# V and K of twelve sequences per class-split layer, moved into the wait for the split; transfers issued later

## The chip, the core and the metric

The kernel runs on one core of a Trainium2 chip. The metric is the device time of one execution in microseconds; a result is the median of several executions. Every trace is of one execution, taken by the hardware profiler.

## What is computed

Sixteen sequences (B) of 512 tokens (S) with 256 channels (C) go through four attention layers, each of the form x = x + attention(layernorm(x)), with 16 heads of 16 dimensions. The order is `PLAN = ("a", "f", "b", "f")`:

```python
x = x + attn_a(layernorm(x))   # causal mask, biases on q, k, v
x = x + ffn(layernorm(x))      # "f": attention within two classes of tokens
x = x + attn_b(layernorm(x))   # rotary positions, no mask
x = x + ffn(layernorm(x))      # "f" again, same weights

# in an "f" layer:
sim = (qg_n * q_n).sum(-1).mean(-1)              # cosine of each token's q with a fixed direction
sim = (sim - sim.min()) / (sim.max() - sim.min())  # over ALL tokens of ALL sequences
pos = sim > 0.9                                  # two classes; the first 5 tokens belong to both
# each token attends to the tokens of its own class and the first 5
```

The 16 sequences of an "f" layer are one batch row set of the same call, so the minimum and the maximum couple them: no product of an "f" layer can start before `sim` of all sixteen sequences is known. This is the class split.

## The kernel before

**Work units.** A quad is one layer, one sequence b and four heads (g = 0 to 3): 256 quads, 64 to a layer. For a quad TensorE (PE) makes the score product twice. First `maxima.score` (tile `s`, L610) gives scores with queries on the partitions, from which VectorE (DVE) takes a row maximum (L619, or the masked L626 in layer 0); the maxima are turned, split in two and written through DRAM (`md`, L654) into extra rows of the quad's Q operand (L657, GpSimd queue). Then `products.score` (tile `t`, L687) gives the shifted scores with keys on the partitions, ScalarE (ACT) takes the exponential (L702) and `weigh` (tile `po`, L713) multiplies with V; `o` (L729) evicts the quad's result. The maxima run 20 score steps (`AHEAD`), that is two and a half quads, ahead of the products.

**Operands through DRAM.** Q and K of a sequence are kept in DRAM (`qd`, `kd`) as high and low parts, V in `vd`. `prep(layer, b, x)` makes them: layernorm (`stats`, `begin`), transposition (`normed`, tile `xp`) into x^T with a high and a low part (`xh`, `xl`), then six-matmul projections for V (`values`, L467, two halves), Q and K (`parts`, L360, two halves each). Each half of Q or K is split into two parts in a tile of a pool of two buffers (`t`, tag "parts": `tq`, `tk`) and sent by four transfers from the SP queue (`send`, L370 and L374). In an "f" layer `prep` also makes `sim` (`similar`, `similarity`): on GpSimd by a power (L432), on ScalarE and VectorE for the last sequence. `constant_rows(b)` (L245) writes 16 constant rows of `qd` and `kd` per head from DRAM, once for each sequence. `load_quad` (L577, GpSimd queue) brings one quad's Q and K into one of five buffers.

**Order.** PE's order is written out by the program: a main loop over the quads calls `advance` (maxima), `score` and `weigh`, and between them `fill_in` runs steps of background generators (`prep`, `tail`, `masked`, `registers`) by a planner with made-up costs and due times (`yield wait, cost`). `tail(layer, b)` divides, projects and adds to x, then pushes `prep(layer + 1, b)`. So while layer n runs its products, layer n + 1 is prepared. The other engines' and queues' orders are set by a scheduler that plays the program through; SP and GpSimd issue their transfers strictly in that order.

**The transition to an "f" layer.** After the last quad of layers 0 and 2 the loop drains all background work (tail of sequence 15, prep of 14 and 15) and calls `split(layer + 1)`: global extremes, classes, four flag rows per sequence to DRAM (`fd`), and from there 64 transfers (L568) into rows of `qd` and `kd` of all sixteen sequences. Then the quads of the "f" layer are loaded, 20 score steps of maxima run, and the first product `t` follows.

Of the kernel before, what the change touches and what calls it, by code (L numbers as in the profile page):

```python
# [63 lines left out]


TURN, ONE, TWO, POOL = 107, 2400, 4000, 6000
ROWS = 48
# [52 lines left out]
def hybrid_kernel(ctx: ExitStack, tc: tile.TileContext, a: dict, out: bass.AP):  # L120
# [4 lines left out]
    def pool(name, bufs, **kw):  # L125
# [5 lines left out]
        pool("w", 2),  # L131
# [15 lines left out]

    def load_const(name, shape, pool_=None):
        t = (pool_ or const).tile(shape, F32, tag=name, name=name)
        nc.sync.dma_start(t, a[name])  # L150
        return t
# [12 lines left out]
    xd = [dram.tile([P, NT, C], F32, tag=f"xd{b}", name=f"xd{b}") for b in range(B)]  # L164
    fd = dram.tile([4, B, S], F32, tag="fd", name="fd")
# [3 lines left out]
    def load_x(layer, b):  # L169
        t = p3.tile([P, NT, C], F32, tag="x", name=f"x{layer}_{b}")  # L170
        src = a["x"][b].rearrange("(t p) c -> p t c", p=P) if layer == 0 else xd[b]
        nc.sync.dma_start(t, src)
        return t
# [7 lines left out]

    def load_weights(layer, project):

        kind = PLAN[layer]
        ws = (WO,) if project else (WQ, WK, WV)
        tag = "o" if project else "q"
        wp = pwo if project else wpool
        wh = wp.tile([P, 2, len(ws), C], FR, tag="wh" + tag, name=f"wh{tag}{layer}")
        wl = wp.tile([P, 2, len(ws), C], FR, tag="wl" + tag, name=f"wl{tag}{layer}")
        for i in ws:  # L190
            raw = ptmp.tile([P, 2, C], F32, tag="tmp", name=f"wraw{layer}_{i}")
            nc.sync.dma_start(raw, a[f"{kind}_w"][:, :, i, :])
            if i in (WQ, WK):
                by_parity = ptmp.tile([P, 2, C], F32, tag="tmp", name=f"wpar{layer}_{i}")
                nc.vector.tensor_scalar(
                    by_parity.rearrange("p c (i e m) -> p (c i) e m", i=2, e=2),
                    raw.rearrange("p c (i m e) -> p (c i) e m", i=2, e=2),
                    SCALE if i == WQ else 1.0,
                    None,
                    ALU.mult,  # L200
                )
                raw = by_parity
            k = 0 if project else i
            nc.scalar.copy(wh[:, :, k, :], raw)
            nc.vector.tensor_tensor(wl[:, :, k, :], raw, wh[:, :, k, :], ALU.subtract)
        return wh, wl

    def broadcast_row(name):
        t = const.tile([P, C], F32, tag=name, name=name)
        nc.sync.dma_start(t, a[name].partition_broadcast(P))  # L210
        return t
# [30 lines left out]
    def constant_rows(b):  # L242
        for w, d in ((0, qd[b]), (1, kd[b])):
            for e in range(2):
                nc.sync.dma_start(d[e, ROWS:], a["zo"][w].unsqueeze(1).to_broadcast([HALF - ROWS, H // 2, S]))  # L245
# [36 lines left out]
    def late_constants():  # L282
        late["later"] = load_const("later", [P, P])
        for kind in ("a", "f"):
            bo[kind] = broadcast_row(f"{kind}_bo")
        late["regs"] = load_const("regs", [P, 3, B * NT])
        late["hm"] = load_const("hm", [P, 2 * H])
        late["blk"] = load_const("blk", [P, H, HV])
        late["half"] = load_const("half", [P, REG])
        for t in rst:  # L290
            nc.gpsimd.memset(t.bitcast(F32), 0.0)
            for e in range(2):
                r = HALF * e + ROWS + 2
                nc.gpsimd.dma_start(t[r : r + 2], a["rows"][e])
        late["cos"] = load_const("cos", [P, S])
        late["sin"] = load_const("sin", [P, S])
        direction()


    def prep(layer, b, x):  # L300
# [35 lines left out]
        def normed(u):  # L336
# [12 lines left out]
            if u == 0:  # L349
                xn(2)  # L350
                xn(3)

# [65 lines left out]
        def similarity():  # L418
# [7 lines left out]
            if b == B - 1:  # L426
# [29 lines left out]
        def values(u):  # L456

            v = vst[b % 2]
# [24 lines left out]

        yield 0, 0
# [16 lines left out]
        for u in range(2):  # L501
            yield lag, 1380
            values(u)
            lag = 0
        if kind == "b":
            for w in "qk":
                for i in range(2):
                    yield (8000 if w == "k" and i == 0 else 0), 1362
                    half_turned(w, i)
                turned(w)  # L510
        elif kind == "a":
            for w in "qk":
                for i in range(2):
                    yield 0, 1362
                    parts(w, i)
        else:
            for w, i in ("q0", "q1", "k0"):
                yield 0, 1362
                parts(w, int(i))
            yield 0, 1750  # L520
            similar()
            yield 0, 1362
            parts("k", 1)
            yield 0, 260
            similarity()
        busy["prep"] -= 1
# [4 lines left out]
    def split(layer):  # L531

        n = B * NT
# [11 lines left out]
        nc.vector.tensor_scalar(dg, ident[:2, :2], mm, None, ALU.mult)  # L545
        pb = small(f"mb{layer}")
# [11 lines left out]
        nc.vector.tensor_tensor(fl[:, 3, :], pos, regs[:, 1, :], ALU.mult)  # L558
        pf = small(f"pf{layer}")
# [5 lines left out]
        for b in range(B):  # L565
            for k, d in ((0, qd[b]), (2, kd[b])):
                for e in range(2):
# [3 lines left out]
                    )  # L571


    def load_quad(i):
        layer, b, g = quads[i]
        for t, d in ((Qs[i % NB], qd[b]), (Ks[i % NB], kd[b])):
            nc.gpsimd.dma_start(t, d[:, :, 2 * g : 2 * g + 2, :].rearrange("e r h s -> (e r) h s"))  # L577
# [12 lines left out]
    def maxima(quad):  # L590
# [10 lines left out]
        def score(t, p):  # L601
# [6 lines left out]
            for e in range(2):  # L608
                r = slice(HALF * e, HALF * e + n_rows)
                nc.tensor.matmul(  # L610
# [123 lines left out]
    def registers(layer, b):  # L734
# [80 lines left out]
        def first():  # L815
            yield (lambda: b == 0 or (layer, b - 1) in NEG), 0
# [3 lines left out]
        def rest():  # L820
            yield (lambda: (layer, b, 0) in registered), 0
# [10 lines left out]
    busy = {"norm": False, "prep": 0, "layers": set(), "first": 0}  # L832
    prepared, registered, summed, tailed, put = set(), set(), set(), set(), set()
    divided = set()
# [36 lines left out]
    def tail(layer, b):  # L871
# [59 lines left out]
        def can():  # L931
# [5 lines left out]
                and (b < 2 or layer + 1 == len(PLAN) or (layer + 1, b - 2) in prepared)  # L937
# [61 lines left out]
    def push_call(f, after=None):  # L999
        def gen():  # L1000
            yield (lambda: busy["prep"] == 0 and (not after or after in tailed)), 0
# [4 lines left out]
    def drain(credit=None, until=None):  # L1006

        while fill and not (until and until()):
            now = clock["now"]
            able = [s for s in fill if s.ready <= now and (s.next == 0 or banks[0] <= now) and s.open()]  # L1010
            if not able:
                if credit is not None:
                    return
# [30 lines left out]
    def prep0(b, x=None):  # L1044
        push(prep(0, b, load_x(0, b) if x is None else x), 2)
        busy["first"] += 1
        constant_rows(b)

    prep0(0, first_x)
    early_constants()  # L1050
# [5 lines left out]
    def advance(to, budget=0):  # L1056

        while taken["n"] < to:
# [10 lines left out]
            if budget:  # L1069
                at = clock["now"]  # L1070
                drain({"ns": budget})
                clock["now"] = max(clock["now"], at + budget)

    waiting = None
    for i, (layer, b, g) in enumerate(quads):
# [4 lines left out]
        if b or g or layer:  # L1080
# [15 lines left out]
        if kind == "a" and g == 1:  # L1096
            push(masked(b), 2)
        if b == 0 and g == NG - 1 and layer + 1 < len(PLAN):
            push_call(lambda layer=layer: W.__setitem__(layer + 1, load_weights(layer + 1, False)))
        if b == 0 and g == NG - 2:  # L1100
            push_call(lambda layer=layer: WP.__setitem__(layer, load_weights(layer, True)), layer and (layer - 1, B - 1))
        if alone:
            advance((2 * NT) * i + AHEAD, 900)
        if i not in put:
            drain(until=lambda: i in put)
        score, weigh = products(i)
        for t in range(NT):
            for p in range(2):
# [3 lines left out]
                if p == 0:  # L1112
                    fill_in(layer)
                elif waiting:
# [5 lines left out]
            if i == 0:  # L1120
                load_through(i + 4) if t == NT - 1 else None
            waiting = lambda weigh=weigh, t=t: weigh(t)
        if kind != "f" and b == B - 1 and g == NG - 1 and layer + 1 < len(PLAN):
# [3 lines left out]
            drain()  # L1127
            split(layer + 1)
# [46 lines left out]
```

## Time and profile before

| | |
|---|---|
| three timed executions | 4234.24, 4244.86, 4248.88 us; median 4244.86 |
| the profiled execution | 4242.52 us, span 4240.7 us |
| busy in the span | PE 3937.4 (93%), DVE 3207.0 (76%), ACT 2631.8 (62%), POOL 1820.8 (43%) |
| mean granted TensorE clock | 0.946 of full speed |
| DMA | 661.84 MB, mean 156 GB/s; mean busy shares of the 16 engines between 0.2 and 1.0 by stage |
| last eviction `o` of layer 0, first product `t` of layer 1 | 1272.5 and 1381.65 us |
| last eviction `o` of layer 2, first product `t` of layer 3 | 3291.4 and 3408.7 us |
| first product `t` of layer 0 | 100.4 us |

Times are from the start of the span. PE is matrix multiplication, PEld its weight loads; POOL is GpSimd; SPq is the SP queue that issues transfers. In a view by windows each row holds the busy time of an engine and in brackets its instructions, then the granted TensorE clock, the mean busy share of the 16 DMA engines and what they moved. The chain of waits is the one path of work that ended last, each row a start, a length and a line.

### The profile page before, as it was taken

To read this page: it belongs to the slowest core of one execution; us is meant where nothing else is said; L and a number is where in the kernel's file an instruction comes from. 1 tells how busy PE (TensorE), PEld (TensorE's weight loads), DVE (VectorE), ACT (ScalarE), POOL (GpSimd) and SP (SyncE) were. 2 spreads that over 40 slices of the span, in tenths; PEclk is the share of its full clock that TensorE was granted. 3 is DMA by queue.
4 is the path that set the end of the run, shared out by engine and by line. 5 is a ranking of instruction groups with operands and counts; after the bars stand their busy time and mean duration, and the time that the engine had idled before them with its cause. 6 is when DMAs were issued, how large, how long until landed. Compare 5 with 4: busy or idle time off the path is not lost.

```text
span 4240.7 us, 79626 instructions
## 1 busy us (share of the span) xinstructions
PE 3937.4 (93%) x27440; PEld 2051.1 (48%) x27440; DVE 3207.0 (76%) x7488; ACT 2631.8 (62%) x5288; POOL 1820.8 (43%) x2421
## 2 busy tenths in 40 slices
PE   3899999999995999999999999999999599999999
PEld 2565656565553444444444444444444334444444
DVE  4676776667654888888888788888886389999996
ACT  1444454444452777777777667777777267777777
POOL 2124545354543256656665634444444412222221
PEclk6899999899996999999999999999999689999999
DMA  9556566666645345555554645455554623333331
GB/s 300 160 159 187 182 200 181 189 184 190 193 128 167 96 137 170 163 149 165 171 162 152 186 146 169 146 167 168 164 157 126 188 85 114 122 116 114 119 121 51
DMA packets 294722, 661.84 MB, mean 156 GB/s; under 512 B 51624, under 2 KB 90032, under 8 KB 294320
## 3 DMA queue, kind: packets, MB, share of 16 engines
q1 hardware_dynamic: 204080, 384.02, 28.9%
q0 software_dynamic: 90240, 272.73, 21.6%
q8 instruction: 219, 3.59, 0.3%
q14 instruction: 183, 1.50, 0.1%
HBM read 379.46 MB, written 298.06 MB: 160 GB/s over the span
## 4 chain that ended last, share of the span: by engine, by line
PE 72%; DVE 10%; DMA 7%; SPq 3%; ACT 3%; issue 3%; POOL 2%; ACTq 0%; DVEq 0%; POOLq 0%
PE po L713 19%; PE s L610 15%; PE t L687 11%; DVE mx L619 5%; PE pv L467 5%; PE pj L922 4%; PE pq L360 4%; DMA qd<-tq 3%; PE pk L360 3%; PE ot L884 2%; POOL nd L432 2%; DVE sc L626 1%; PE rs L759 1%; PE t L698 1%; SPq L568 1%
## 5 line engine op out<-in xcount | busy, mean ns | idle before, releaser
L702 ACT ACTIVATE e<-t 128x512 f32<-128x512 f32 (+2 forms) x3840 | 2017.6, 588 | 824.2 <-PE t L687 538.6
L619 DVE TENSOR_REDUCE mx<-s 128x1 f32<-128x512 f32 x3072 | 1944.4, 681 | 334.7 <-PE s L610 326.2
L610 PE MATMUL s<-ks,qs 52*128 52x512 f32 (+4 forms) x4096 | 1030.8, 481 | 92.3 <-DMA ks<-kd 78.1
L687 PE MATMUL t<-qs,ks 52*128 52x512 f32 (+4 forms) x4096 | 1000.2, 402 | 103.5 <-ACT e L702 35.5
L713 PE MATMUL po<-e,v 128*32 128x512 f32 (+1 forms) x8192 | 1031.1, 576 | 5.1 <-ACT o L729 3.9
L610 PEld LDWEIGHTS s<-ks,qs 48*128 48x128 f32 (+1 forms) x4096 | 429.9, 191 | 1085.7 <-ACT e L702 310.9
L687 PEld LDWEIGHTS t<-qs,ks 50*128 50x128 f32 (+1 forms) x4096 | 496.8, 191 | 302.3 <-DVE mx L619 102.6
L626 DVE CUSTOM_DVE_ANT_0 sc<-s,mask_s_bf 128x128 bf16<-128x128 f32 (+3 forms) x1024 | 497.7, 486 | 160.5 <-PE s L610 78.6
L577 POOL DMA_DIRECT2D qs<-qd x256 | 153.6, 601 | 811.5 <-PE t L687 530.7
L657 POOL DMA_DIRECT2D qs<-md x512 | 268.5, 529 | 543.7 <-DMA md<-ms 516.2
L432 POOL TENSOR_TENSOR nd<-nd,nhalf 128x16 f32<-128x16 f32 x120 | 346.1, 2902 | 22.5 <-DVE nd L423 22.5
L713 PEld LDWEIGHTS po<-e,v 128*32 128x32 f32 x8192 | 162.6, 109 | 271.9 <-issue 194.3
L309 POOL TENSOR_SCALAR xn<-x,nm,st 128x256 f32<-128x256 f32 x256 | 141.4, 557 | 117.7 <-PE xp L340 111.1
L698 PE MATMUL t<-mask_t_bf 64*128 64x128 bf16 x2048 | 189.4, 234 | 0.0
L380 POOL CAST tq<-yq 128x512 fp32r<-128x512 f32 x80 | 49.1, 613 | 267.9 <-DMA qd<-tq 92.5
L884 PE MATMUL ot<-ident,o 128*128 128x128 f32 x1024 | 148.2, 288 | 16.3 <-DVE tq L399 7.1
L577 POOL DMA_DIRECT2D ks<-kd x256 | 140.1, 548 | 52.1 <-issue 14.5
L729 ACT COPY o<-po 128x512 f32<-128x512 f32 x256 | 153.3, 599 | 7.4 <-PE po L713 7.0
L884 PEld LDWEIGHTS ot<-ident,o 128*128 128x128 f32 x1024 | 117.1, 146 | 47.8 <-DVE mx L619 10.1
L340 PE MATMUL xp<-ident,xn 128*128 128x128 f32 x512 | 89.1, 299 | 46.0 <-POOL xn L309 43.7
L930 DVE TENSOR_TENSOR x<-pj,x 128x512 f32<-128x512 f32 x128 | 87.1, 680 | 55.0 <-PE pj L922 50.5
L347 ACT CAST xh<-xp 128x512 fp32r<-128x512 f32 x128 | 76.0, 595 | 84.1 <-PE xp L340 83.9
(358 smaller groups left out, 4991.6 us busy)
## 6 DMA issues: line engine op xcount, KB each, us to landing
qs<-qd POOLq DMA_DIRECT2D x256, 512.0 KB, 4.5
ks<-kd POOLq DMA_DIRECT2D x256, 512.0 KB, 5.3
qd<-tq SPq DMA_DIRECT2D x256, 256.0 KB
kd<-tk SPq DMA_DIRECT2D x256, 256.0 KB
vd<-vst SPq DMA_DIRECT2D x64, 576.0 KB
v<-vd SPq DMA_DIRECT2D x64, 576.0 KB
qd<-tq SPq DMA_DIRECT2D x256, 128.0 KB
kd<-tk SPq DMA_DIRECT2D x256, 128.0 KB
```

What stands on the lines that cost most here:

```text
L360: nc.tensor.matmul(dst, ww[:, c, w, cols], xx[:, c, :], start=(k == 0 and c == 0), stop=(k == 2 and c == 1))
L432: nc.gpsimd.tensor_tensor(nd[:, 0, t], nd[:, 0, t], nhalf[:, t], ALU.pow)
L577: nc.gpsimd.dma_start(t, d[:, :, 2 * g : 2 * g + 2, :].rearrange("e r h s -> (e r) h s"))
L610: nc.tensor.matmul(st["ps"][e][:, (p % m) * end :][:, :end], q[r, p, t * P : (t + 1) * P], k[r, p, :end], start=True, stop=True,)
L619: nc.vector.tensor_reduce(st["mx"][:, e, p, t : t + 1], st["ps"][e], AX.X, ALU.max, negate=True)
L626: nc.vector.tensor_tensor_reduce(w, st["ps"][e][:, (i % m) * end :][:, :end], late["mask_s"][:, S - end :], 1.0, -3.0e38, ALU.add, ALU.max ...
L657: nc.gpsimd.dma_start(q[r : r + 2], d[:, e].rearrange("k j t p -> k j (t p)"))
L687: nc.tensor.matmul(ps[e], k[rows[e], p, t * P : (t + 1) * P], q[rows[e], p, q0:], start=True, stop=(kind != "a"),)
L698: nc.tensor.matmul(ps[e][:, :P], mk[:, 0], mk[:, 1], start=False, stop=(o == 1))
L702: st["exp", t] = nc.scalar.activation(e_[:, : m * w], st["ps"][e][:, : m * w], AF.Exp)
L713: mm = nc.tensor.matmul(st["po"][32 * j : 32 * j + 32, q0:], v[:, t, h * HV : h * HV + 32], E.pop((t, j)), start=(t == 0), stop=(t == NT - 1),
L884: nc.tensor.transpose(ps[:, g * P : (g + 1) * P], O[layer, b, g][:, t * P : (t + 1) * P], ident)
```

## The change

1. For the "f" layers, `prep` of sequences 4 to 15 (`HELD = 4`) makes no K and no V. It writes `xh` and `xl` to DRAM (`keep`: `xtd`, two transfers of 512 KB on SP) and pushes a generator `rest` that opens when the layer before has ended (`busy["late"]`). `rest` loads the two back (GpSimd queue), into the idle weight set of the other layer or into `xh`, `xl` buffers, and makes K and V. The weights' two sets become fixed tiles (`wsets`) for that.
2. `split` becomes a generator run by the planner among the `rest` steps; it waits only for `similarity` of sequence 15 (`compared`). After it the planner goes on with background work for `LAND` = 16000 planner ns. What is left of the `rest` steps runs between the first scores of the "f" layer.
3. Only sequence 0's flags (4 transfers) are written at the split; those of sequence 1 follow at the first quad, of b + 2 during sequence b (`flags`).
4. `constant_rows` of sequence b + 2 is called during sequence b of layer 0, no longer with `prep0`.
5. `behind` gives transfers (loads of constants, weights, x, quads, x^T, constant rows, flags) a wait for the latest score matmul `at["pe"]` written before them.
6. `sim` of sequence 14 is also made on ScalarE and VectorE. Within `prep`, V comes after Q and K. A tail may start when the prep two sequences back has been transposed (`taken_up`) rather than finished. The first quads of an "f" layer are loaded one by one. In layer 0 `fill_in` runs after the products of a step.

```diff
+    def behind(dma):
+        if at["pe"] is not None:
+            tc.add_manual_dep(
+                dma.ins,
+                at["pe"].ins.name,
+                mybir.DependencyInfo(mybir.DependencyClass.Sync, mybir.DependencyReason.DATA),
+                reason="in order of use",
+            )
+        return dma
...
+    xtd = {
+        b: [dram.tile([P, 2, S], F32, tag=f"xt{k}{b}", name=f"xt{k}{b}") for k in "hl"] for b in range(HELD, B)
+    }
...
-            if b == B - 1:
+            if b >= B - 2:
                 nc.scalar.activation(nd[:, 0], nd[:, 0], AF.Sqrt)
...
+        def rest():
+            yield (lambda: layer in busy["late"] and (not busy["room"] or busy["prep"] < 2)), 0
+            room = not busy["room"]
+            st["vst"] = int(room)
+            if room:
+                busy["room"] = True
+                st["xh"], st["xl"] = (
+                    w.rearrange("p a b c -> p (a b c)")[:, : 2 * S].rearrange("p (c s) -> p c s", c=2)
+                    for w in wsets[(layer + 1) % 2]
+                )
+            else:
+                busy["prep"] += 1
+                st["xh"] = p2.tile([P, 2, S], FR, tag="xh", name=f"xh{n}_")
+                st["xl"] = p2.tile([P, 2, S], FR, tag="xl", name=f"xl{n}_")
+            for k, d in zip(("xh", "xl"), xtd[b]):
+                behind(nc.gpsimd.dma_start(st[k], d))
+            yield 8000, 1362
+            parts("k", 0)
+            yield 0, 1362
+            parts("k", 1)
+            for u in range(2):
+                yield 0, 1380
+                values(u)
...
+            prepared.add((layer, b))
+
+        def keep():
+            for k, d in zip(("xh", "xl"), xtd[b]):
+                nc.sync.dma_start(d, st[k].bitcast(F32))
...
-            for w, i in ("q0", "q1", "k0"):
+            held = b >= HELD
+            if held:
+                keep()
+            for i in range(2):
+                yield lag, 1362
+                parts("q", i)
+                lag = 0
+            if not held:
                 yield 0, 1362
-                parts(w, int(i))
-            yield 0, 1750
+                parts("k", 0)
+            yield (2 * ONE if held else 0), 1750
             similar()
...
+            yield (2 * TWO if held else 0), 260
             similarity()
+            compared.add((layer, b))
+            if held:
+                busy["layers"].remove(layer)
+                push(rest(), 4)
+                return
...
-        for b in range(B):
-            for k, d in ((0, qd[b]), (2, kd[b])):
-                for e in range(2):
+        flags(0)
+        splits.add(layer)
+
+    def flags(b):
+        for k, d in ((0, qd[b]), (2, kd[b])):
+            for e in range(2):
+                behind(
                     nc.sync.dma_start(
...
     def load_quad(i):
...
-            nc.gpsimd.dma_start(t, d[:, :, 2 * g : 2 * g + 2, :].rearrange("e r h s -> (e r) h s"))
+            behind(nc.gpsimd.dma_start(t, d[:, :, 2 * g : 2 * g + 2, :].rearrange("e r h s -> (e r) h s")))
...
-                and (b < 2 or layer + 1 == len(PLAN) or (layer + 1, b - 2) in prepared)
+                and (b < 2 or layer + 1 == len(PLAN) or (layer + 1, b - 2) in taken_up)
...
     def prep0(b, x=None):
         push(prep(0, b, load_x(0, b) if x is None else x), 2)
         busy["first"] += 1
-        constant_rows(b)
...
+        if layer == 0 and (i == 0 or g == 2 and b + 2 < B):
+            constant_rows(b + 2 if i else 1)
...
+        if kind == "f" and (alone or g == 2 and b + 2 < B):
+            flags(1 if alone else b + 2)
...
-            drain()
-            split(layer + 1)
+            busy["late"].add(layer + 1)
+            drain(until=lambda: (layer + 1, b) in compared)
+            push(split(layer + 1), 0)
+            drain(until=lambda: layer + 1 in splits)
+            due = clock["now"] + LAND
+            drain(until=lambda: clock["now"] >= due)
```

## The prediction

> **What bounds the kernel now.** I read the page's slices first: PE's and the DMA engines' rows show three places where PE is not nine tenths busy (the start, slices 13 and 33).
>
> ```profile
> PE   3899999999995999999999999999999599999999
> PEclk6899999899996999999999999999999689999999
> DMA  9556566666645345555554645455554623333331
> ```
>
> Then windows, of a stretch inside layers 0, 2 and 3, and of the first transition:
>
> ```profile
> 680.00:980.00 300.00, 281.47 (x2319) 179.83 (x2318) 205.19 (x764) 146.61 (x308) 145.35 (x174) 0.93 0.60 181
> 2760.00:3060.00 300.00, 295.61 (x1888) 142.30 (x1884) 247.59 (x472) 216.20 (x425) 140.15 (x162) 1.00 0.52 163
> 3700.00:4000.00 300.00, 295.97 (x2057) 127.26 (x2060) 274.37 (x497) 231.59 (x469) 72.07 (x145) 1.00 0.37 115
> ...
> 1320.00:1340.00 20.00, 2.06 (x7) 1.02 (x7) 6.92 (x20) 3.10 (x4) 5.51 (x9) 0.53 0.70 187
> 1340.00:1360.00 20.00, 10.20 (x29) 5.36 (x29) 10.21 (x18) 1.66 (x4) 3.70 (x14) 0.50 0.84 295
> 1360.00:1380.00 20.00, 14.60 (x63) 6.88 (x61) 17.04 (x32) 1.46 (x4) 1.29 (x3) 0.50 0.20 60
> ```
>
> Inside layers 0 and 2 PE is the bound (94% and 99% busy, DVE 68% and 83%); at the transition it idles or runs at half clock. Third, the chain of waits over that transition:
>
> ```profile
> 1295.89 8.63 POOL nd L432 x3
> ...
> 1315.19 0.59 ACT tk L401
> ...
> 1320.74 3.75 DMA qd<-tq
> 1324.59 0.59 ACT tk L401
> ...
> 1329.76 3.00 DMA fd<-fs
> ...
> 1376.64 1.56 DMA md<-ms
> 1378.71 2.81 DMA qs<-md
> 1381.65 1.29 PE t L687 x2
> ```
>
> A power on GpSimd, Q and K tiles that wait for their pool's transfers, the flags' 64 issues, and the maxima's transfer behind them: 109 us from the last eviction (1272.5) to the first `t`; 117 in layer 3 (3291.4 to 3408.7). Last, the start:
>
> ```profile
> 33.47 8.43 DMA kd<-tk
> 41.92 8.14 DMA qd<-in_zo
> 100.37 1.01 PE L687 MATMUL t<-qs,ks 50*128 50x512 f32 x2 [18.11 <-DVE g L262]
> ```
>
> Constant rows of all sequences fill the DMA engines (share 0.98, 1.09, 1.00, 0.89 in the four windows from 20 to 100 us, 302, 387, 344 and 286 GB/s, mean 330).
>
> The sum is made against the profiled execution, 4242.5 us (span 4240.7), 2.4 below the median. Anything within 0.3% (12.7 us) can't be told from no change.
>
> **1. V and K leave the layers' bodies.** In the timeline of PE a V takes 2.87 us at full clock (1281.24 to 1284.11), a K two times 1.37: 5.6 us a sequence. By the order of PE's instructions before and after, V and K of ten sequences (4 to 13) move out of the body of layer 0 and of layer 2; those of 14 and 15 stood behind the last product already. 56 us of PE work leave each body. How much time that is: between two like layers, 1 and 3, a sequence takes 60.5 and 51.7 us (four evictions), and layer 3 lacks layer 2's preparation, some 9.3 us of PE work by the same rows: 8.8 for 9.3, 0.94. Layer 0 is 94% busy. So 56 x 0.94 = 53 a body, **-105** for both. In layer 2 a sequence goes from 59.6 (2702.3 to 2762.0) to 54.3, with DVE at 49.5 of it (247.6/5): still PE's. Bounds: if layer 2 stops near layer 3's pace with DVE at 91% (49.5/0.91 = 54.4) nothing is lost; if half of layer 0's saving falls to the transfers that its chain also shows, -80; above, -112. The two writes of x^T per sequence go onto SP between other sends, at a DMA share of 0.6 from which three times their bytes are gone: nothing, unless SP's head waits there (then see the rival of held transfers).
>
> **2. The transition is filled.** Twelve `rest` steps bring 67 us of PE work. What else stands between the last eviction and the first `t`, from the timeline of PE at full clock: transposes of tail and x^T 5.3, projection 2.8, two Qs 5.5, two `sq` and `st` 4.5, split 2, 40 score matmuls of 0.245 9.8, registers 4, together some 34; the last half V falls behind the first `t`. PE needs about 99, less where the trace counts its overlaps twice: 96. The split's own chain shortens from 109 to about 83: the power of sequence 14 (11.5 us) goes to ACT and DVE, V and K of 15 (8, at half clock) leave, 4 flags instead of 64 precede the maxima's transfer (7 to win, since the 20 score steps end at 1374.7 anyway). It no longer decides. Transfers: a `rest` reads 1024 KB and writes 1536 KB of K and 576 of V. Up to the first `t`, SP's and GpSimd's orders hold ten and a half of these (33.7 MB by the transfers' sizes), two Qs (3.1), two x^T (2.1), x and V (1.6) and four quads (4.2): 45 MB. At the start's mean of 330 GB/s that is 136 us, at its best window's 387, 116. Third, every half K passes the pool of two: in the chain above three such tiles (two `tk` L401, a `tq` on GpSimd between) take 9.4 us with the engines half idle, 3.1 each: 25 tiles are 78 us; with landings of 8.4 instead of 3.75 us, as at the start, a tile's turn grows from 6.2 to 10.9 us, 5.4 each, and they take 135. So the ends are 96 and 150, PE alone and everything slow; I take 124, between the transfers' two rows. That is **+15** on 109 and **+7** on 117, where the work of part 1 has found its place: filled time, not saved time.
>
> The Trainium skill (DMA: Bandwidth & Descriptors, "Issuing engines are not separate DMA queues") says that transfers started by SP and by GpSimd run on the same 16 engines, and its Specifications give about 358 GB/s for HBM per core. That speaks against piling 45 MB into the wait: 126 us by that figure, an estimate, for my 124; the window with 387 here exceeds it. The skill (TensorE: Matmul & The Clock Gate, Part 1) also has the clock halve after an idle window of some 3.4 us; the rows with 0.50 above agree, and a filled wait would then run at full clock.
>
> **3. The start.** Constant rows of 13 sequences (1024 KB each) no longer stand before the first maxima's transfer: `ms` is ready at 66.4, `md` is issued only at 88.4. The 20 score steps run from 55.2 to 82.3. Without the queue `t` follows at 82.3: -18. The first K load also waits 8.1 us for constant rows and 8.4 for a landing that is 3.75 elsewhere, so scores start some 9 earlier: **-26** (-10, if V of sequence 1 or its K is late next, to -32). The rows are written later at a share near 0.6: hidden; their 4 issues a sequence are 2.5 us of SP, beside the products.
>
> **4. Held transfers and small edits.** A wait for a score matmul is put before SP's and GpSimd's loads; both queues issue in order, so `md` sends, Q and K sends, and quad loads stand behind. For quads GpSimd waits today for `t` of the buffer's last quad (531 us in all), which PE makes after the score named: no new wait. For flags, x and constants SP may wait where it did not: between 0 and the 4.5 us of a quad's landing for some tens of the 64 sequences, partly hidden by 20 score steps; nearest is the existing slack of SP, 1049 us of waiting for maxima. I take **+8** (0 to 25), which includes the spill of the last `rest` into the "f" layers. Flags spread over the sequences, `taken_up` and the new order of V: nothing; they lie beside 12 us quads.
>
> Sum: -105 + 22 - 26 + 8 = -101: 4141.5 in the profiled execution, 4144 as a median.
>
> **The rivals.** *The wait becomes transfers* (0.2): each transition takes 150 to 158, the slow end of part 2: +37 on average over my 124 is +60 in all, 4205. For: 45 MB and the pool of two; against: 387 GB/s was seen. *The bodies give half* (0.1): chain, not PE, sets layers 0 and 2 (its stretch of layer 0 holds 11% of transfers of Q and K parts): -52 instead of -105, 4197. Against: 94 to 99% busy. *Held transfers stall the products, slower* (0.14): place: SP's head in every layer, a load waiting for a score while `md` of the next quad stands behind it. Price: one landing of 4.5 us a sequence, 64 times 4.5 = 288, from which 101 go: 4432; it decides from 101/64 = 1.6 us a sequence. For: SP is one queue for all sends; against: 20 score steps, 25 us, lie between `md` and its use. *All cancels* (0.04): holds near that point. That the move is not made can't be: the order of PE's instructions shows it.
>
> **How the numbers follow.** My case has 0.52, centre 4144, own range 4085 to 4190 (bodies -112 to -80, transitions 100 to 140, start -32 to -10, holds 0 to 25, not all at one end). The faster rivals end at 4205 and 4197. Low end 4075, since waits of 96 with full bodies give 4242 - 112 - 34 - 32 = 4064; high end 4245, which leaves out most of the slower case. Faster 0.82, same 0.04, slower 0.14.
>
> **What would show it.** Right: first `t` of layer 0 near 74; per sequence 67 to 69 us in the second half of layer 0 (74 now) and 54 in layer 2; between last eviction and first `t` 124 us with DMA shares near 1 and the clock at 1.0; 51.7 unchanged in layer 3. Wrong: bodies at the old pace; PE stalls for ks, qs or x in steady layers; transitions above 150.

## The result, and the profile after

The median went from 4257.31 to 4275.34 us (20 executions each, 4234.24 to 4266.76 and 4255.57 to 4290.17): 1.0043 times the time before, with a 95% interval from 1.0029 to 1.0058. The change makes the kernel slower by about 18 us (0.4%), above the forecast of 4144 and above its range, which ended at 4245. The profiled execution after has 4278.88 us and a span of 4277.1.

Single executions of either kernel lie up to 35 us apart. The profiled one of before is 14.8 us below the median of its twenty, that of after 3.5 above: of the +36.4 between the two spans below, some 18 come from that. Each row of the tables is one execution, so a few us in one stage show nothing by themselves.

Cut at the first product `t` of a layer (timeline of PE) and at the last eviction `o` of a layer (timeline of ACT), the two spans compare as follows; a "body" runs from the first `t` to the last `o`, a "wait" from the last `o` to the next `t`.

| us | start | body 0 | wait 1 | body 1 | body 2 | wait 2 | body 3 | span |
|---|---|---|---|---|---|---|---|---|
| before | 100.4 | 1172.1 | 109.2 | 949.1 | 960.6 | 117.3 | 819.5 | 4240.7 |
| after | 65.2 | 1154.2 | 160.7 | 942.1 | 946.1 | 162.6 | 833.5 | 4277.1 |
| difference | -35.2 | -17.9 | +51.5 | -7.0 | -14.5 | +45.3 | +14.0 | +36.4 |
| forecast | -26 | -53 | +15 | 0 | -53 | +7 | 0 | -101 |

(The forecast's +8 for held transfers had no place of its own. The rest of the span is the tail, 12.5 us in both.)

The slices of the page show the same at a glance: the start is better, and the dips of PE are wider, with the DMA row at 6 and 8 where it was 4 and 5 (slices 12 and 13), and at 9 where it was 6 (slice 32).

```profile
PE   6899999999986999999999999999998699999999
PEclk7899899799898999999999999999999899999999
DMA  6556666466668445555455655544445943333332
```

The windows (busy time of PE, PEld, DVE, ACT and POOL with their instructions, then the granted clock, the DMA share and GB/s) answer to those of before: first the stretches inside layers 0, 2 and 3, then three pieces of the first wait.

```profile
680.00:980.00 300.00, 282.11 (x2153) 174.25 (x2153) 206.63 (x750) 134.99 (x288) 140.82 (x166) 0.86 0.60 187
2760.00:3060.00 300.00, 280.84 (x1688) 122.31 (x1684) 241.31 (x459) 204.70 (x403) 139.30 (x160) 0.93 0.45 145
3700.00:4000.00 300.00, 290.59 (x2029) 125.85 (x2026) 274.63 (x484) 226.00 (x455) 70.80 (x143) 1.00 0.37 116
...
1260.00:1280.00 20.00, 13.17 (x63) 9.45 (x62) 3.91 (x11) 4.37 (x9) 2.11 (x4) 0.83 1.03 338
...
1300.00:1320.00 20.00, 5.52 (x26) 4.62 (x24) 2.09 (x4) 3.42 (x6) 2.48 (x6) 0.68 1.04 353
...
1360.00:1380.00 20.00, 12.17 (x47) 7.14 (x46) 9.68 (x17) 3.87 (x8) 2.46 (x6) 0.70 0.67 200
```

Two things are new. In layer 2 PE is busy for 280.84 of 300 us where it was for 295.61, and its granted clock has fallen from 1.00 to 0.93: something else holds it up. (It does fewer instructions, 1688 for 1888, because V and K have left; the pace stays near 60 us a sequence.) And in the wait PE is not the bound that "filled" promised: in the piece from 1300 it is busy for 5.5 of 20 us while the DMA engines are at 1.04. From 1220 to 1380 as a whole PE is busy for 114.82 of 160 us, the engines' mean share is 0.92 and the granted clock 0.83. The chain of waits in the first wait is a row of transfers of K parts:

```profile
1227.80 5.88 DMA kd<-tk
...
1238.53 8.64 DMA qd<-tq
...
1263.52 11.80 DMA kd<-tk
...
1287.64 6.71 DMA qd<-tq
...
1311.32 7.95 DMA kd<-tk
```

The view of transfers over the whole wait, 1220 to 1380, gives the bytes and the mean rate:

```profile
DMA packets 19354, 47.09 MB, mean 294 GB/s; under 512 B 2604, under 2 KB 2892, under 8 KB 19344
```

The chain in layer 2 shows what holds PE there, once in every sequence (here one case; 2785.24, 2844.83, 2904.00 and 3026.20 are the same):

```profile
2963.13 0.43 PE s L694 x2
...
2963.79 0.61 PE xp L365 x4
...
2964.94 5.71 POOL nd L458 x2
2970.65 1.95 DMA qs<-md
...
2972.74 1.26 PE t L771 x2
...
2974.85 1.86 PE po L797 x8
```

GpSimd's power for `sim` (`nd`), then the transfer of the maxima into the Q operand, then the product; the eight `po` matmuls after it take 1.86 us where they take 0.99 at full clock. The timeline of GpSimd around the same place shows why a power can delay a transfer: the transfer is issued from the same engine, behind it.

```profile
2959.16 11.53 POOL L458 TENSOR_TENSOR nd<-nd,nhalf 128x16 f32<-128x16 f32 x4 [1.54 <-DVE nd L449]
2970.65 1.09 POOL L741 DMA_DIRECT2D qs<-md  x2
```

The chain of the start has lost the constant rows (`qd<-in_zo`), and the landing of the first K parts is 5.8 us instead of 8.4:

```profile
29.60 5.78 DMA kd<-tk
...
36.07 4.40 DMA ks<-kd
...
58.99 4.38 DMA g<-in_g
...
65.21 0.92 PE t L771 x2
```

### The profile page after: what moved, and what is told of

Its sections match the earlier page's. It is cut to its first block, busy times and chain, and to the rows that moved or that the text cites. A ratio compares the mean times of both kernels' runs of the same rounds, so it can differ in the third digit from the quotient of the medians.

```text
span 4277.1 us, 80049 instructions
## 1 busy us (share of the span) xinstructions
PE 3987.2 (93%) x27440; PEld 2076.4 (49%) x27440; DVE 3241.9 (76%) x7492; ACT 2627.8 (61%) x5290; POOL 1819.6 (43%) x2459
## 4 chain that ended last, share of the span: by engine, by line
PE 69%; DVE 11%; DMA 10%; POOL 3%; issue 3%; ACT 2%; SPq 2%; DVEq 0%; POOLq 0%; ACTq 0%
PE po L797 19%; PE s L694 14%; PE t L771 11%; PE pj L1009 4%; PE pq L386 4%; DVE mx L703 4%; DMA kd<-tk 3%; DVE sc L710 3%; POOL nd L458 2%; PE pv L493 2%; PE ot L971 2%; PE pk L386 2%; DMA qd<-tq 2%; PE rs L843 2%; DMA x<-in_x 2%
## 5 line engine op out<-in xcount | busy, mean ns | idle before, releaser
L771 PE MATMUL t<-qs,ks 52*128 52x512 f32 (+4 forms) x4096 | 1019.8, 407 | 99.2 <-DMA qs<-md 31.6
L694 PE MATMUL s<-ks,qs 52*128 52x512 f32 (+4 forms) x4096 | 1046.1, 479 | 64.1 <-DMA ks<-kd 29.8
L797 PE MATMUL po<-e,v 128*32 128x512 f32 (+1 forms) x8192 | 1051.4, 586 | 6.0 <-ACT e L786 3.1
L771 PEld LDWEIGHTS t<-qs,ks 50*128 50x128 f32 (+1 forms) x4096 | 507.3, 192 | 307.5 <-DVE mx L703 113.1
L458 POOL TENSOR_TENSOR nd<-nd,nhalf 128x16 f32<-128x16 f32 x112 | 323.2, 2904 | 37.7 <-DVE nd L449 37.5
L782 PE MATMUL t<-mask_t_bf 64*128 64x128 bf16 x2048 | 201.0, 236 | 0.0
L428 DVE TENSOR_TENSOR tk<-pk,tk 128x512 fp32r<-128x512 f32 x64 | 44.0, 689 | 175.2 <-ACT tk L427 168.1
L427 ACT CAST tk<-pk 128x512 fp32r<-128x512 f32 x64 | 37.5, 587 | 185.0 <-DMA kd<-tk 114.7
```

The lines of the kernel that those rows point to most:

```text
L458: nc.gpsimd.tensor_tensor(nd[:, 0, t], nd[:, 0, t], nhalf[:, t], ALU.pow)
L694: at["pe"] = nc.tensor.matmul(st["ps"][e][:, (p % m) * end :][:, :end], q[r, p, t * P : (t + 1) * P], k[r, p, :end], start=True, stop=True,)
L771: nc.tensor.matmul(ps[e], k[rows[e], p, t * P : (t + 1) * P], q[rows[e], p, q0:], start=True, stop=(kind != "a"),)
L782: nc.tensor.matmul(ps[e][:, :P], mk[:, 0], mk[:, 1], start=False, stop=(o == 1))
L797: mm = nc.tensor.matmul(st["po"][32 * j : 32 * j + 32, q0:], v[:, t, h * HV : h * HV + 32], E.pop((t, j)), start=(t == 0), stop=(t == NT - 1),
```

## The experiments

All ratios are to the kernel before, run on the same chip. The table cuts each experiment's profiled execution like the one above.

| us | start | body 0 | wait 1 | body 1 | body 2 | wait 2 | body 3 | span |
|---|---|---|---|---|---|---|---|---|
| e1_held16 | 66.0 | 1215.2 | 97.4 | 955.7 | 948.6 | 92.9 | 847.8 | 4236.1 |
| e2_after_mult | 64.8 | 1123.2 | 158.0 | 950.6 | 881.3 | 158.7 | 836.3 | 4185.7 |
| e3_before_mult | 99.1 | 1162.1 | 100.4 | 947.4 | 959.3 | 100.8 | 816.7 | 4198.9 |
| e4_before_zo | 75.8 | 1180.9 | 108.0 | 951.2 | 963.0 | 117.0 | 817.4 | 4225.8 |
| e5_mdsp | 65.3 | 1150.9 | 161.7 | 948.8 | 884.0 | 159.8 | 838.3 | 4221.4 |
| e6_xfree | 66.0 | 1111.0 | 155.1 | 945.5 | 942.8 | 161.3 | 818.4 | 4212.7 |
| e7_p4x3 | 66.5 | 1097.0 | 162.5 | 954.9 | 950.5 | 163.8 | 854.3 | 4262.2 |
| e8_mdsp_h10 | 67.0 | 1187.2 | 127.0 | 957.6 | 916.4 | 124.2 | 843.2 | 4235.2 |
| e9_both | 65.6 | 1089.7 | 157.5 | 939.0 | 884.6 | 158.9 | 820.4 | 4128.4 |
| e10_both_held16 | 65.6 | 1147.0 | 95.8 | 953.6 | 938.2 | 90.6 | 825.1 | 4128.7 |
| e11_both_p4x3 | 66.1 | 1070.9 | 164.0 | 948.3 | 888.7 | 163.8 | 822.1 | 4136.6 |

**1. Everything but the move of V and K.** With `HELD = 16` no sequence's V and K wait; the rest of the change stays.

```diff
-HELD = 4
+HELD = 16
```

> The changed kernel with HELD = 16: V and K of all sequences are made in the bodies again, nothing is held back for the wait; start, flags, holds and the other edits stay. Theory (the waits grew from 109 and 117 us to 161 and 163 because 45 MB and 25 part tiles pass through them): the waits fall to 85 to 105 us, the start stays at 65 us, bodies of layers 0 and 2 return to about 1170 and 960 us, in sum 35 to 65 us below the kernel before. Rival (held transfers stall the bodies): bodies of layers 0 and 2 are longer than the kernel before's by 20 us or more each, and the total is at or above the kernel before.

Measured: 4235.47 us, ratio 0.9956 (0.9941 to 0.9971). Without the move the kernel is 20 us faster than before, less than the 35 to 65 expected; with it, slower. The move costs the waits 63 and 70 us and gives the bodies 61 in layer 0, only 2.5 in layer 2; bodies 1 and 3 are 14 shorter each. It is not the only part that cost time: body 0 is 1215.2 here, 43 us longer than before the change where about 1170 was expected, and body 3 is 28 longer. So of the rival, held transfers that stall the bodies, the part on layer 0 came true, those on layer 2 and on the total did not (see experiments 6 and 10).

**2. The power in the kernel after, replaced by a multiplication.** The same shapes go through GpSimd; one `nd` instruction takes 0.22 us instead of 2.9.

```diff
-nc.gpsimd.tensor_tensor(nd[:, 0, t], nd[:, 0, t], nhalf[:, t], ALU.pow)
+nc.gpsimd.tensor_tensor(nd[:, 0, t], nd[:, 0, t], nhalf[:, t], ALU.mult)
```

> The changed kernel with the power on GpSimd in similarity (4 of 2.9 us a sequence) replaced by a multiplication of the same tiles; the similarity values are others then. Theory (the power stands ahead of the maxima's loads on GpSimd's queue and stalls PE once a sequence): layer 2 falls from 59 to 61 us a sequence to 54 to 56, layer 0 by 2 to 5 us a sequence, total 60 to 110 us below the changed kernel. Rival (PE is not what bounds layers 0 and 2, or the held transfers are): pace of layer 2 stays within 1.5 us of 60, total within 25 us of the changed kernel.

Measured: 4197.17 us, ratio 0.9865 (0.9846 to 0.9885). Body 2 falls by 65 us and body 0 by 31; a sequence of layer 2 takes 53.2 us, near the 54 of the forecast. So the saving of layer 2 exists and GpSimd's power had eaten it. The total falls by 78 us.

**3. The same replacement in the kernel before.** It tells whether the power was already in the way.

> The kernel before with the same replacement of the power. Theory (in the order of before the power is hidden behind PE's work in the bodies): layer 2 stays at 59 to 60 us a sequence; only the transitions lose some 10 us each, total 10 to 35 us below the kernel before. Rival (the power costs the same in both): layer 2 falls by 3 us a sequence or more, total 60 us below or more.

Measured: 4208.74 us, ratio 0.9894 (0.9877 to 0.991). Body 2 does not move (959.3 for 960.6): before the change the power was hidden there. The waits fall by 9 and 16 us and body 0 by 10, in all 47 us, more than the 35 expected. GpSimd issued maxima's transfers behind a power before the change as well (four powers from 2883.33, 11.53 us long, a transfer at 2895.99), but there the chain of layer 2 holds no `nd` at all. The change moved where the power falls between PE's steps, and it took away PE work that covered it; what the cover was worth is read from experiments 1, 9 and 10 below.

**4. The late constant rows alone, in the kernel before.**

```diff
-        constant_rows(b)
...
+    constant_rows(0)
...
+        if layer == 0 and (i == 0 or g == 2 and b + 2 < B):
+            constant_rows(b + 2 if i else 1)
```

(with the wait for a score matmul on these transfers, as in the change.)

> The kernel before, with one part of the change: constant rows of sequence b + 2 are called during sequence b and wait for the latest score matmul. Theory (the start's 35 us come from these transfers): first t at 65 to 80 us instead of 100, everything else as before, total 20 to 35 us below. Rival (the rows only move their cost into the body of layer 0, or the late loads of constants are what matters): first t above 90, or the body of layer 0 longer by what the start gains; total within 10 us.

Measured: 4235.83 us, ratio 0.9949 (0.9932 to 0.9966). The first `t` comes at 75.8 instead of 100.4, 24.6 earlier. Body 0 is 9 us longer in this one execution; that the rows are not quite hidden later is likely, but 9 us are too few to show it.

**5. The maxima's rows loaded from SP's queue instead of GpSimd's, in the kernel after.** The power stays where it is; only the transfer no longer stands behind it.

```diff
-nc.gpsimd.dma_start(q[r : r + 2], d[:, e].rearrange("k j t p -> k j (t p)"))
+nc.sync.dma_start(q[r : r + 2].bitcast(F32), d[:, e].rearrange("k j t p -> k j (t p)"))
```

> The changed kernel with the two loads of the maxima's rows per quad (md into the Q operand) issued from SP instead of GpSimd; all else equal, nothing left out. Theory (in the changed order the power of 4 x 2.9 us stands on GpSimd ahead of a load that the next product needs, which is why the bodies gave 33 of 105 us): layer 2 at 53 to 56 us a sequence, layer 0 20 to 35 us shorter, waits still 155 to 163, total 50 to 100 us below the changed kernel. Rival (the power costs through something else than this queue, such as the similarity being late): layer 2 stays at 58 to 61 us a sequence.

Measured: 4231.4 us, ratio 0.9946 (0.9922 to 0.997). Body 2 is 884.0, as with the multiplication, and no other stage moves by more than 7 us. Body 0 falls by 3 us where 20 to 35 were expected, and the total by 44 where it was 50 to 100: in layer 0 this order alone costs little as long as x is held (experiments 6 and 9). The window of layer 2 is back at full clock with PE at 99%:

```profile
2760.00:3060.00 300.00, 297.30 (x1919) 131.15 (x1918) 271.07 (x520) 230.31 (x458) 137.34 (x137) 1.00 0.50 157
```

POOL is as busy as without the edit (137 us for 139), so it was the order on its queue, not its load, that cost 62 us.

**6. The load of x without its wait for a score matmul, in the kernel after.**

```diff
-        behind(nc.sync.dma_start(t, src))
+        nc.sync.dma_start(t, src)
```

> The changed kernel without the wait for a score on the loads of x. Theory (in the changed kernel x arrives later, GpSimd's addition of the output bias, 2.4 us, falls on VectorE's short operation on 5 partitions in layer 3, which then takes 1.7 instead of 0.4 us and stalls PE): in layer 3 that operation is 0.4 us again and a sequence 51.7 instead of 52.7 us, layer 1 perhaps 60.5 instead of 59.4. Rival (flags and quad loads that wait make layer 3 slower): layer 3 stays at 52.5 us or more.

Measured (one execution): 4214.45 us. Body 0 falls by 43 us and body 3 by 15, to the pace of before (51.7 us a sequence); body 2 stays (946.1 to 942.8), and layer 1 stays at 59.4 us a sequence, where a return to 60.5 had been thought possible. In layer 0 the kernel after had x on its chain. The steps are, in two stretches of that chain:

```profile
517.16 3.81 DMA x<-in_x
521.00 0.53 DVE bs L344 x2
```

```profile
1036.67 9.30 DMA x<-in_x
1045.99 0.75 DVE bs L344 x2
```

The load is issued behind the sends of Q and K parts on SP, and layernorm waits for all of its landing; over 300 to 1150 us it is 5.7% of the chain, 48 us. The loss in layer 3 is told under "what was not expected".

**7. Three tiles instead of two for the Q and K parts (and seven instead of nine for the exponentials, to make room).**

```diff
-        pool("p4", 2),
-        pool("pe", 9),
+        pool("p4", 3),
+        pool("pe", 7),
```

> The changed kernel with three tiles instead of two in the pool of parts; to make room the pool of exponentials has seven instead of nine tiles. Theory (the DMA engines bound the waits, 47 MB in 160 us): both waits within 10 us of 161 and 163, landings longer. Rival (the turn of the two tiles bounds the waits): waits at or below 145 us.

Measured (one execution): 4263.99 us. The waits do not move: 162.5 and 163.8. The transfers in the first wait (1163 to 1323) are, to the packet, those of the kernel after in the same time:

```profile
DMA packets 19354, 47.09 MB, mean 294 GB/s; under 512 B 2604, under 2 KB 2892, under 8 KB 19344
```

So the turn of the two-tile pool does not set the wait, though the chain above reads as if it did: each link is a landing. That the landings are long because the engines are nearly full is read from their mean share, 0.90 here and 0.92 in the kernel after. Body 0 does fall, by 57 us, and body 3 grows by 21; why body 3 grows stays open.

**8. Half as many sequences moved, with the maxima's rows on SP.** `HELD = 10` on the kernel of experiment 5.

> The changed kernel with the maxima's loads on SP and HELD = 10: V and K of six sequences instead of twelve are held back. Theory (a wait holds some 95 us of chain, in which about 30 MB pass for nothing): waits of 95 to 115 us, bodies of layers 0 and 2 some 34 us longer each than in the run with 12 held sequences and these loads on SP, total 20 to 70 us below that run and 70 to 120 us below the kernel before. Rival (each held sequence costs its 5.5 us in the wait from the first on): total within 15 us of that run.

Measured: 4245.21 us, ratio 0.998 (0.9963 to 0.9998). The waits are 127.0 and 124.2, above the 95 to 115 expected of a wait with room for six sequences, and the total is 14 us above that of experiment 5, where the rival had set its bound at 15. From none moved (97.4) to six (127.0) it is 4.9 us a sequence, from six to twelve (161.7) 5.8: there is no free room for six, which cost nearly as much as the six after them. No run moves fewer than six. The windows of the first wait, in four equal parts, show why room is left and yet not used:

```profile
1254.00:1286.00 32.00, 28.26 (x169) 23.12 (x169) 12.62 (x34) 10.62 (x19) 19.89 (x20) 0.95 0.86 278
1286.00:1318.00 32.00, 24.80 (x132) 19.36 (x131) 7.84 (x22) 8.94 (x18) 5.51 (x8) 0.91 0.91 293
1318.00:1350.00 32.00, 4.26 (x30) 3.79 (x29) 3.35 (x5) 4.70 (x7) 1.93 (x5) 0.61 0.74 208
1350.00:1382.00 32.00, 25.05 (x56) 11.69 (x56) 26.10 (x45) 2.34 (x7) 4.29 (x12) 0.50 0.34 100
```

The moved work fills the first half; then the split's own chain runs nearly alone, at half clock, with the engines at 0.74 and 0.34. By the timeline the flags (`fd`) go out 82.9 us after the last eviction, and the first `t` follows 44.1 later. In the kernel of experiment 10, where nothing is moved, they go out at 52.4, and `t` follows 43.4 later. In the second wait the delay is on both sides: 64.5 and 59.7 here, 46.8 and 43.8 in experiment 10. The moved work has not been laid beside the chain; it has pushed the chain back or stretched it.

**9. Both repairs together** (experiments 5 and 6).

> The changed kernel with both repairs at once: the load of x waits for no score matmul, and the maxima's rows are brought into the Q operand from SP's queue instead of GpSimd's. Theory that the bodies lost their saving to the order on the queues, each loss in its own place: layer 0's body near 1111, layer 2's near 884, layer 3's near 818, waits unchanged near 155 and 160, sum about 66 + 1111 + 155 + 945 + 884 + 160 + 818 + 13 = 4152 us. Rival, that SP's queue now holds both the loads of x and the maxima's rows and they meet there: layer 0's body back above 1140 or layer 2's above 910, 4190 us or more.

Measured: 4129.75 us (4128.59 to 4130.29), ratio 0.9698 (0.9669 to 0.9727). Body 0 falls by 64.5 us, more than the 43 and 3 of the two alone: once x is free, the order of the maxima's rows gives another 21 there (experiments 6 and 9). Body 2 falls by 61.5. The waits stay. In the slices of its page PE is at nine tenths or more everywhere but at the start and in the two waits:

```profile
PE   5999999999987999999999999999998699999999
```

**10. Both repairs, and no sequence moved** (`HELD = 16`).

> As the run with both repairs, but no sequence's V and K are moved (HELD = 16). Theory that a moved sequence costs in the wait what it saves in the body (5 to 5.7 us against 5.6 of PE work): waits near 97 and 93, bodies of layers 0 and 2 near 1111 + 56 = 1167 and 945, layer 3 near 818, sum about 66 + 1167 + 97 + 945 + 945 + 93 + 818 + 13 = 4144, within 20 us of the run with both repairs. Rival, that the move does pay once the queues are clear: the run with both repairs is faster than this one by 30 us or more.

Measured: 4140.72 us (4130.49 to 4141.69), ratio 0.9719 (0.9692 to 0.9746); the spans of the two profiled executions are 4128.7 and 4128.4. The ratios' intervals overlap. On the same chip the four executions of experiment 9 (4128.59 to 4130.29) all lie below the four of this one, whose profiled execution is its fastest; the medians are 11 us apart. So the move gains at most some 11 us of the 83 forecast for it (105 less 22), and with four executions each even that is not firm. The waits without the move leave the engines half idle:

```profile
1212.00:1244.00 32.00, 22.91 (x132) 17.28 (x131) 14.10 (x36) 11.59 (x21) 21.30 (x19) 0.88 0.59 173
1244.00:1276.00 32.00, 13.31 (x65) 8.95 (x63) 9.00 (x19) 6.64 (x11) 7.51 (x8) 0.71 0.78 223
1276.00:1308.00 32.00, 23.76 (x52) 10.57 (x52) 24.82 (x42) 1.39 (x4) 4.50 (x13) 0.50 0.35 106
```

Between 10 and 9 stands the price list of the move with the queues clear: body 0 -57.3, body 2 -53.6, waits +61.7 and +68.3, bodies 1 and 3 -14.6 and -4.7 (that the last two belong to the move was not tried apart). The sum is -0.2 us, between two single executions.

**11. Both repairs and the pool of three.**

> Both repairs, and the pool of the Q and K parts has three tiles instead of two (the exponentials' pool seven instead of nine). Theory that in layer 0 the pool's turn and the late load of x are one and the same loss, a preparation that comes late: layer 0's body stays near 1090 us (1075 to 1100), waits stay at 157 and 159 since the DMA engines set them, total 4115 to 4150. Rival, that the pool's turn is a loss of its own: layer 0's body falls by another 30 us or more, to 1060 or less, total below 4110.

Measured: 4133.79 us, ratio 0.9706 (0.9686 to 0.9726), the same as experiment 9. Body 0 falls by 19 us where the pool alone had given 57, to 1070.9, between the 1075 of the theory and the 1060 of the rival: two thirds of what the pool gave was already gained by the two repairs. That this common part is one loss, a preparation that comes late, fits and is argued. The rest is given back in the waits (+6.5 and +4.9), body 1 (+9) and body 2 (+4).

## Why the prediction was wrong

Three steps failed: the wait's term of +15 and +7 us (part 2), the clearance "still PE's" for layer 2 (part 1), and the +8 for held transfers (part 4). The forecast sum was -101, the spans say +36: 137 us apart (the medians, +18, 119). By terms of the spans, the bodies of layers 0 and 2 miss by 73 us, the waits by 75, and the start is 9 better; the term of +8 for the holds against +7 in bodies 1 and 3 makes up the last one.

**Part 1, V and K leave the bodies: the size was right, the clearance wrong.** 53 us a body was the price on PE, and experiments 9 and 10 measure 57.3 and 53.6. In layer 0 the move gave 61 us in the kernel after, too (experiment 1); the hold on x hid it (part 4), and a sequence of the second half took 72.6 us instead of 67 to 69 (66.7 in experiment 9). In layer 2, what failed is the sentence that nothing else is late: "still PE's" was judged by busy shares of PE and DVE, and GpSimd, at 47% in that stretch, was not looked at as a queue. It has four powers of 2.9 us in one go (11.53 us from 2959.16), and issues the maxima's transfer behind them (2970.65). Before, PE's own work covered that; with 5.6 us a sequence less, it stood bare, and the 53 us came back as 5.7 us of `nd` on the chain in each sequence. Experiments 2 and 5 show this for layer 2 from two sides, the duration and the order. The cover is shown by the table: with V and K in the bodies the two repairs shorten body 2 by 10.4 us (948.6 in experiment 1, 938.2 in experiment 10), without them by 61.5 (946.1 in the kernel after, 884.6 in experiment 9). In experiment 1 `nd` still makes up 5.9% of the chain from 2700 to 3100, 24 us, at next to no cost: a chain names a path, not what its removal would give. In layer 0 the account is not closed: the multiplication gives 31 us, the order alone 3.

**Part 4, held transfers: the term was mis-sized.** +8 us stood for all of them, with SP's slack as the nearest row. The hold on x alone costs 43 us in layer 0 (61.2 with the maxima's rows on SP, experiments 5 and 9) and 15 in layer 3. The text looked for the price on SP's head, as `md` delayed behind a load. It was the load itself that came too late: x opens a preparation, and a preparation has no 20 score steps of cover in front of it. The slower rival named the right mechanism at the wrong place, and at a price (288 us) several times too high.

**Part 2, the filled wait: wrong in its rate and in its overlap.** 45 MB was a good count (47.09), the 124 us were not: this mix of loads and sends took 160, which is 294 GB/s, with the engines at a mean share of 0.92. Even at a share of 1.0 it would take some 147 (an estimate, 0.92 of 160). Why the rate was lower than at the start was not tried. The 330 GB/s came from the start, where constant rows filled the engines; of eight windows of 20 us in the wait two reach that (338 and 353), and its ends, at shares of 0.82 and 0.67, have 256 and 200. Taking a value below that row's own 136 us had no reason but the better window. The Trainium skill's 358 GB/s (DMA: Bandwidth & Descriptors, Specifications) would give an estimate of 126; none of these eight windows exceeds 353. The full clock that was expected of a filled wait did not come either: it was 0.83. The faster rival, "the wait becomes transfers", with 150 to 158, was near for both waits; the pool of two, which it also named, is cleared by experiment 7.

The second error is in the word "filled". The forecast let the split's chain shorten to 83 and then vanish beneath the moved work. It does shorten: with nothing moved, the waits are 95.8 and 90.6 for 109.2 and 117.3. But it does not lie beneath. Its links, K loads, flags, maxima, go through the same queues and engines as the moved sequences. In the kernel after, the flags go out 70.3 us behind the last eviction (52.4 in experiment 10), the first score of layer 1 stands at 100.9 (65.1), the maxima's transfer at 141.0 (84.7) and the first `t` at 160.7 (95.8): each link has grown, and 47 of the 65 us come behind the flags. So the baseline that the moved work is to be compared with is not 109 but 96, and in each wait it costs 62 to 70 us on top. That six sequences cost about 5 us each and six more nearly 6 is measured. Which of the sends ahead of the flags on SP, the slower landings, and the `rest` steps between the first scores stretches each link was not tried by itself.

**Part 3, the start: right**, with -35 (3 beyond its bound) for -26 in the change and -24.6 for the constant rows alone; the remaining 10 come from the rest of the change and were not taken apart. Whether the rows are hidden later stays open, with 9 us more in body 0 of one execution.

**"Layer 3 unchanged 51.7"** failed at 52.7 us a sequence, by the mechanism below.

Two slips leave the sum as it is: the second dip of PE stands in slice 32, not 33, and 150 to 158 us over 124 are +30 a wait on average, not +37; the +60 for both is right.

With both repairs, the kernel lands at 4129.75 us, near the forecast, and that is not its confirmation but luck: the start gives 35 and the bodies 168 (158 of them in layers 0 and 2), the waits take 90. Of the 158 the move gives 111; the other 47 are there without it (experiment 10 against before) and were not taken apart.

## What to carry to other kernels

Before work is moved off the engine that sets the pace, list for every in-order queue what stands ahead of each transfer, and how much of the moved work was its cover: a load that waits behind a slow instruction of its issuing engine cost little here until the cover went. A wait into which work is moved is only free for what the waiting chain does not itself use; price the chain's links at the loaded rate, and measure the slope with half of the move. Holding a transfer back until it is near its use pays for what crowds others (the constant rows) and costs for what opens a chain (x).

## What was not expected of the hardware

A small VectorE instruction took four times as long beside an addition of two tensors on GpSimd. In layer 3, the registers' correction (5 partitions by 256) stands as follows in the groups of VectorE from 3600 to 4200 us (busy, mean ns): before, after, and with the load of x not held (experiment 6).

```profile
L896 DVE SCALAR_TENSOR_TENSOR on<-on,neg 5x256 f32<-5x256 f32 x12 | 4.8, 403 | 0.0
```

```profile
L983 DVE SCALAR_TENSOR_TENSOR on<-on,neg 5x256 f32<-5x256 f32 x11 | 18.2, 1658 | 0.0
```

```profile
L983 DVE SCALAR_TENSOR_TENSOR on<-on,neg 5x256 f32<-5x256 f32 x11 | 4.4, 403 | 0.0
```

In the timelines of GpSimd and VectorE after, one such case:

```profile
3699.52 2.37 POOL L967 TENSOR_TENSOR x<-x,f_bo 128x1024 f32<-128x1024 f32 x1 [3.17 <-DMA x<-xd]
```

```profile
3700.38 1.79 DVE L983 SCALAR_TENSOR_TENSOR on<-on,neg 5x256 f32<-5x256 f32 x1
```

GpSimd's addition ends at 3701.89 and VectorE's instruction 0.28 us later: it did little until GpSimd was done. The Trainium skill (SBUF — State Buffer, "SBUF: two separate sides") says that a VectorE instruction with two inputs in SBUF and a GpSimd instruction that reads SBUF share a port pair, which the one that starts first holds for its whole duration; these rows agree. So does the other order: at 1794.39, in layer 1 after, VectorE's instruction began 0.20 us before such an addition and took its 0.40 us.

The held x brings GpSimd's addition onto that instruction. By the timelines, thirteen of the fifteen corrections of layer 3 overlap with an addition in the kernel after, none before or in experiment 6. Over all thirteen kernels, body 3 takes 817 to 825 us where none overlaps (x not held) and 834 to 854 where thirteen or more do (x held). VectorE is 92% busy in layer 3, so that one microsecond a sequence is a microsecond of pace.

In layer 1 the mean of the same instruction fell from 1136 to 466 ns in the same view from 1450 to 2250 us, but the addition of x is not what it met there before: that is a product of the rotation of K (`yk`, 1.28 us, for example at 1792.30), and only one of the fifteen met the addition. Body 1 does not follow this mean: it is 942.1 us in the kernel after and 945.5 in experiment 6, where the mean is no higher.

The other is the cost of a power on GpSimd: 2.9 us for 128 by 16 elements, 0.22 for a multiplication of the same shape (experiment 2).
